# Last terms along w made inside the attention's first turns, position terms in row halves, q and k weights loaded two pairs ahead

## The chip, the cores and the metric

The kernel runs on one core of a Trainium2 chip. Its time is device microseconds of one execution. Its engines work beside each other: TensorE (PE in the profile; PEld is its weight load), VectorE (DVE), ScalarE (ACT), GpSimd (POOL), and SyncE (SP), whose queue issues nearly all DMAs, in order.

## The reference

Four layers follow each other on an input of 48 x 48 tokens with 768 channels, all in f32. Only the first, a transformer block, is touched; and of that, its attention:

```python
xn = layernorm(x, ln1_g, ln1_b)
qkv = xn.reshape(B, H * W, C) @ qkv_w + qkv_b              # 12 heads of 64
attn = jnp.einsum('bqc,bkc->bqk', q * scale, k)            # 2304 x 2304 for each head
rel_h = jnp.einsum('bhwc,hkc->bhwk', r_q, Rh)              # r_q is q as 48 x 48 rows; Rh, Rw are
rel_w = jnp.einsum('bhwc,wkc->bhwk', r_q, Rw)              # tables of relative positions
attn = attn + rel_h[:, :, :, :, None] + rel_w[:, :, :, None, :]
out = softmax(attn) @ v
```

Then come the projection, the residual, a second layernorm and the MLP. The other layers (two in the frequency domain, one of iterated convolutions) are as they were.

## The kernel before

**q, k and v.** `qkv_phase` goes through the tokens in three blocks of 768 (`sb`, three of `NSB`). Each product of 768 x 768 is made from seven half-size products instead of eight; their weights are prepared in the first block and kept in DRAM (`wqk_d`, `wv_d`). In a later block `v_rows` makes v first (L166), and `q_and_k` then makes q and k for six pairs of heads (`pr`, 128 channels each; L297). A pair's weights are one tile of 1344 KB, of which three are held. `v_weights` loads those of pairs 0 and 1; those of the others are loaded where the pair begins (L277). q, k and v go to DRAM (`q_d`, `k_d`, `v_d`). In the last block, after pair 1, `ahead(0)` loads the one-hot matrix and the first pair's keys and values for the attention (L331).

**Position terms.** For every query and head there are 48 terms along h and 48 along w. Each is f32, and is split by two ACT casts and two DVE subtractions into three bf16 parts whose sum it is (`split`, L369). One step of `rel_w` (four columns w, all pairs; L395) or `rel_h` (four rows h of one token half, two pairs; L409) is four f32 matmuls, eight passes on TensorE, followed by one split. A block has 12 steps of each kind. A step's table (192 KB, four held) is loaded by SP up to three steps ahead. `advance()` takes the next step: eight are taken between the passes of pairs 2 to 5, the rest in the next block's `v_rows`. In the last block the rest stands behind the last pair: the 4 last steps along h, then the 12 along w. The parts go to DRAM (`rh_d`, `rw_d`), from where the attention reads them.

**The bound.** Also behind the last pair, a small matmul (L477) yields a bound on the scores, from which `flag` follows. It chooses between `attention_bounded`, which runs here, and `attention_any`. What is inside the branch cannot mix with what is outside.

**The attention.** It works on a pair of heads at a time, one in partitions 0 to 63 and one in 64 to 127. The queries come in five chunks of 464 (the last has 448), the keys in 18 tiles of 128, three to a turn (`KB`). So there are 6 x 5 x 6 = 180 turns, numbered `i`. A turn is: three keys' products q.k (L576, f32, contraction over 64 rows, so that the two heads use the two row halves of the array), the terms for the same three (L585: a one-hot bf16 matrix of 120 rows times the bias tile of 120 rows, added in PSUM onto the product), exp on ACT (L587), row sums of the exps on DVE (L595), and the values of the turn before (L606, f32, 64 columns for each head). At a chunk's end the sums are added over partitions (L614), inverted (L616) and multiplied in (L622), into `oT`, the attention's output. [...]

`load_bias` lays out a chunk's bias tile: 120 rows are 48 for w (16 columns x 3 parts) and 72 for h (24 rows x 3 parts), for both heads, two halves of the key rows and three groups of columns. A chunk's loads are put into SP's queue when the chunk before begins; the next pair's keys and values at the pair's second chunk. Every sixth turn from the third on, a step of `weight_sums` is taken (`other`), which loads later weights, combines them on POOL and stores them; it uses slots of the exps' tile `p`, of which there are ten.

Of the kernel before, what the change touches and what calls it, by code (L numbers as in the profile page):

```python
# [20 lines left out]
P = 128  # L21
# [160 lines left out]

def qkv_phase(tc, ident, x, qkv_w, qkv_b, relT, rel_d, ln_g, ln_b, q_d, k_d, v_d, rw_d, rh_d, wqk_d, wv_d, flag, home, ahead):
# [18 lines left out]
    with (  # L202
# [67 lines left out]
        def q_and_k(sb, have_q, step):  # L270
# [4 lines left out]
            for pr in range(NC):  # L275
                if sb:
                    if (sb, pr) not in wqks:  # L277
                        load_qk(sb, pr)
                    w = wqks.pop((sb, pr))
                else:  # L280
                    w = w_tile(f"wqk_{sb}_{pr}").rearrange("p (n c f) -> p n c f", n=7, c=NC2)
                    wb = wp.tile([P, NC2, P], F32, tag="wb", name=f"wb_{pr}", bufs=2)
                    lo, hi = slice(pr * P, (pr + 1) * P), slice(C + pr * P, C + (pr + 1) * P)
                    nc.sync.dma_start(w[:, 0:2].rearrange("p a c f -> p (a c) f"), wv[:, :, lo])
                    nc.sync.dma_start(w[:, 6], wv[:, NC2:, hi])
                    nc.sync.dma_start(wb, wv[:, :NC2, hi])
                    combine(nc.gpsimd, (w[:, 0], w[:, 1], wb, w[:, 6]), w[:, 3], w[:, 2], w[:, 5], w[:, 4])
                    made.append(w)
                    if pr:
                        nc.sync.dma_start(wqk_d[pr - 1], made[pr - 1])  # L290
# [40 lines left out]
                if pr == 1 and sb + 1 == NSB:  # L331
                    ahead(0)
# [9 lines left out]
        with tc.tile_pool(name="qkv_v0", bufs=1, side="right") as vp:  # L342
            w = vp.tile([P, 7, NC2, TB], F32, tag="wv", name="wv")
            a21 = vp.tile([P, NC2, TB], F32, tag="a21", name="a21")
            load_x(0, 0)
            for k in range(2):
                nc.sync.dma_start(w[:, k], wv[:, k * NC2 : (k + 1) * NC2, 2 * C : 2 * C + TB])
            prepare(0, 0)
            load_x(0, 1)
            nc.sync.dma_start(w[:, 6], wv[:, NC2:, 2 * C + TB :])  # L350
            nc.sync.dma_start(a21, wv[:, :NC2, 2 * C + TB :])
            vb = load_bcast(nc, kp, qkv_b[2 * C : 3 * C], C, "vb")
            qkb = load_cols(nc, kp, qkv_b[0 : 2 * C], 2 * NC, "qkb")
            kb = kp.tile([P, NC], F32, tag="kb", name="kb")
            rel = qp.tile([P, 2, 2 * G - 1], F32, tag="rel", name="rel")
            for s in range(2):
                nc.sync.dma_start(rel[s * HD : (s + 1) * HD], relT)
            qms, kms = (qp.tile([P, NC, NSB], F32, tag=n, name=n) for n in ("qms", "kms"))
            prepare(0, 1)
            combine(nc.gpsimd, (w[:, 0], w[:, 1], a21, w[:, 6]), w[:, 3], w[:, 2], w[:, 5], w[:, 4])  # L360
            sums(0)
            V.tensor_scalar(kb, qkb[:, NC : 2 * NC], HD**-0.5, None, ALU.mult)
            v_rows(0, lambda n: w[:, n])
            nc.sync.dma_start(wv_d, w)

        with tc.tile_pool(name="qkv_o", bufs=1, side="right") as op:
            R = 2 * G

            def split(ps, parts, n):  # L369

                r = op.tile([P, TB], F32, tag="rest", name=f"rest_{n}", bufs=2)
                r = r[:R].rearrange("p (a b c) -> p a b c", a=ps.shape[1], b=ps.shape[2])
                nc.scalar.copy(parts[0], ps)
                V.tensor_tensor(r, ps, parts[0], ALU.subtract)
                nc.scalar.copy(parts[1], r)
                V.tensor_tensor(parts[2], r, parts[1], ALU.subtract)
# [7 lines left out]
            def position_terms(sb, q):  # L384


                q6 = q.rearrange("p c b (j w h) -> p c b j w h", j=KJ, w=KTW)
# [6 lines left out]
                def rel_w(g):  # L394

                    if g == 0:
                        tiles["rw"] = op.tile([P, 3, NC, 2, TB], BF16, tag="rw", name=f"rw_{sb}")
                    d, at = tiles.pop(("w", g)), tiles["rw"]
                    ps = pm.tile([P, 512], F32, tag="m", name=f"rw_{sb}_{g}")
                    pv = ps[:R, :TB].rearrange("p (c b w h) -> p c b w h", c=NC, b=2, w=4)  # L400
                    j, w0 = divmod(4 * g, KTW)
                    for i in range(4):
                        nc.tensor.matmul(pv[:, :, :, i, :], lhsT=d[:, i, :], rhs=q6[:, :, :, j, w0 + i, :], start=True, stop=True)
                    cols = slice(j * P + w0 * KTH, j * P + (w0 + 4) * KTH)
                    split(ps[:R, :TB].rearrange("p (c b t) -> p c b t", c=NC, b=2), [at[:R, n, :, :, cols] for n in range(3)], f"w{sb}_{g}")
                    if g == G // 4 - 1:
                        store(rw_d, at, slice(0, NC * TS))
# [23 lines left out]
                for g in range(G // 4):  # L431
                    steps.append((lambda g=g: load(("w", g), 1, g), lambda g=g: rel_w(g)))
# [33 lines left out]
            rm = qp.tile([P, 2], F32, tag="rm", name="rm")  # L466
            V.tensor_reduce(rm, rel, axis=AX.X, op=ALU.max, apply_absolute_value=True)
            V.tensor_scalar(km, km, rm[:, 0:1], rm[:, 1:2], ALU.add, ALU.add)
            pz = qp.tile([P, 2, NC], F32, tag="pz", name="pz")
            V.memset(pz, 0.0)  # L470
# [3 lines left out]
            onec = qp.tile([P, 1], F32, tag="onec", name="onec")  # L474
            V.memset(onec, 1.0)
# [5 lines left out]
            for _ in range(4):  # L481
                advance()
            inner.close()
            for _ in range(5):
                advance()
            ahead(1)
# [22 lines left out]

def queries(qc):  # L510

    return slice(qc * QB, min(T, (qc + 1) * QB))


def load_onehot(nc, pool, oneh_d, o):

    f = pool.tile([P, 3, P], F32, tag="onehf", name="onehf")
    nc.sync.dma_start(f[:NBR], oneh_d)
    nc.vector.tensor_copy(o[:NBR], f[:NBR])


def attention_loads(nc, q_d, k_d, v_d, rw_d, rh_d):
# [7 lines left out]
    def chunk(qb, c):  # L530
        pr, qc = c
        q = queries(qc)
        n = q.stop - q.start
        nc.sync.dma_start(qb[0][:, :n], q_d[pr * P : (pr + 1) * P, q])
        for s in range(2):
            load_bias(nc, qb[1][:, s, :, :, :n], rw_d, rh_d, 2 * pr + s, q.start, n)
# [4 lines left out]
def attention_bounded(tc, ahead, oT, beside, load_next):  # L541
# [14 lines left out]
    with (  # L556
# [22 lines left out]
        def scores(c, kt):  # L579
# [4 lines left out]
            for s in range(2):  # L584
                nc.tensor.matmul(ps[:, s, :n], lhsT=oneh[:NBR, b % 3, :], rhs=held(c)[1][:NBR, s, b // 3, j, :n], start=False, stop=True)  # L585
# [39 lines left out]
        other = beside(op, lambda name: pp.tile([P, 2, QB], F32, tag="p", name=name).rearrange("p a c -> p (a c)")[:, : 2 * TB].rearrange("p (a c) -> p a c", a=2))  # L625
        for i in range(len(work) + 1):
            if i % 6 == 3:
                next(other, None)
            if i == len(work) - 8:
                load_next()  # L630
            if i < len(work):
                c, k0 = work[i]
                pr, qc = c
                if k0 == 0:
                    nxt = (pr, qc + 1) if qc + 1 < NQB else (pr + 1, 0)
                    if nxt[0] < NC:
                        load_chunk(held(nxt), nxt)
                    if qc == 1 and pr + 1 < NC:
                        load_keys_values(kvs[(pr + 1) % 2], pr + 1)
                for kt in range(k0, k0 + KB):  # L640
                    products(c, kt)
                for kt in range(k0, k0 + KB):
                    scores(c, kt)
            if i:
# [3 lines left out]
                for kt in range(k0, k0 + KB):  # L648
                    values(c, kt)
                if k0 + KB == NT:  # L650
                    finish(c)
        for _ in other:
# [3 lines left out]
def attention_any(tc, ident, oneh, q_d, k_d, v_d, rw_d, rh_d, oT, beside, load_next):  # L656
# [4 lines left out]
    GQ = 2  # L661
    with tc.tile_pool(name="an_o", bufs=2) as op:
# [3 lines left out]
    with (  # L666
# [9 lines left out]
        nc.vector.memset(ones, 1.0)  # L676
        ka = cp.tile([HD, T], F32, tag="ka", name="an_ka")
# [633 lines left out]
def block_kernel(ctx: ExitStack, tc: tile.TileContext, a: dict):  # L1311
# [20 lines left out]
    oneh = atc.tile([P, 3, P], BF16, tag="oneh", name="oneh")  # L1332
# [4 lines left out]
    def load_ahead(stage):  # L1337
        if stage == 0:
            load_onehot(nc, atc, a["oneh"], oneh)
# [5 lines left out]
        qbs = [(pool.tile([P, QB], F32, tag=f"qt{i}", name=f"qt{i}"), pool.tile([P, 2, 2, KJ, QB], BF16, tag=f"bt{i}", name=f"bt{i}")) for i in range(2)]  # L1345
        loads[1](qbs[0], (0, 0))
        ones = pool.tile([P, HD], F32, tag="ones", name="ones")
        nc.vector.memset(ones, 1.0)
# [14 lines left out]
    pw, pw_close = opened("pw", [P, 2, NC2, TB], "right")  # L1363
    load_pw = lambda: nc.sync.dma_start(pw, ps_d[:, :2])
    bounded = nc.values_load(flag)
    with tc.If(bounded > 0) as which:
        attention_bounded(tc, ahead, oT, beside, load_pw)
    with which.Else():
        attention_any(tc, ident, oneh, q_d, k_d, v_d, rw_d, rh_d, oT, beside, load_pw)
# [487 lines left out]
```

## Time and profile before

| | us |
|---|---|
| median of 3 runs | 3815.2 (3811.54 to 3820.01) |
| profiled execution | 3815.61 |
| its span, first to last instruction | 3813.4 |
| mean granted TensorE clock | 0.987 of full |

The profile's page divides the span into 40 slices of 95.3 us. Each digit is the busy share of a slice in tenths:

```profile
PE   7999979999999999998999999999999998999998
DVE  6655455656566666565424433232325567995455
ACT  1323244444444444420310120011013356222342
DMA  7655563333332322124334534443454402112345
```

The attention is the stretch from the sixth slice to the eighteenth, in which ACT is at 4. Its matmuls and exps stand in the page's list of groups: line, engine, operation, output <- inputs, shape, count, then busy time and mean of one:

```profile
L576 PE MATMUL s<-qt,kv 64*128 64x464 f32 (+1 forms) x2160 | 467.8, 565 | 7.6 <-ACT p L587 5.4
L606 PE MATMUL av<-p,kv 128*64 128x464 f32 (+1 forms) x2160 | 456.3, 557 | 0.0
L585 PE MATMUL s<-bt,oneh 120*128 120x464 bf16 (+1 forms) x1080 | 241.3, 359 | 0.0
L587 ACT ACTIVATE p<-s 128x928 f32<-128x928 f32 (+1 forms) x540 | 467.9, 940 | 681.5 <-PE s L585 575.1
```

An f32 matmul is two passes, and each counts as one. A duration is that of one pass, from its start to its modelled end, and passes overlap; their pace is read from their starts.

### The profile page before, as it was taken

How to read it: one execution, taken by the hardware profiler on the slowest of the kernel's cores; microseconds unless marked ns; L12 is line 12 of the kernel's file. 1: busy time of each engine (PE TensorE's matmuls, PEld its weight loads, DVE VectorE, ACT ScalarE, POOL GpSimd, SP SyncE). 2: the span in 40 equal slices, each digit the busy share in tenths (PEclk: the TensorE clock that was granted, in tenths of full speed). 3: DMA queues.
4: the chain of work that ended last, by engine and by line, in shares of the span. 5: the costliest groups of instructions: out<-in, count | busy, mean ns of one | idle time of the engine just before them, and what ended most of it. 6: DMA issues, size and time to landing. Idle time of an engine off the chain costs nothing.

```text
span 3813.4 us, 51839 instructions
## 1 busy us (share of the span) xinstructions
PE 3707.4 (97%) x20914; PEld 2168.0 (57%) x20914; DVE 2032.0 (53%) x3070; ACT 1135.3 (30%) x1803; POOL 653.5 (17%) x498
## 2 busy tenths in 40 slices
PE   7999979999999999998999999999999998999998
PEld 4666543333333333345555555555568876996685
DVE  6655455656566666565424433232325567995455
ACT  1323244444444444420310120011013356222342
POOL 3101001111111111025000000000013301981131
PEclk9999989999999999999999999999999999999999
DMA  7655563333332322124334534443454402112345
GB/s 261 209 191 190 182 189 121 114 108 114 102 101 90 101 90 76 50 86 156 133 105 134 172 109 126 134 133 108 125 161 110 112 29 94 40 33 73 98 117 154
DMA packets 276271, 460.28 MB, mean 121 GB/s; under 512 B 50909, under 2 KB 228821, under 8 KB 269527
## 3 DMA queue, kind: packets, MB, share of 16 engines
q1 hardware_dynamic: 266215, 435.94, 37.5%
q10 hardware_dynamic: 9808, 20.94, 1.5%
q8 instruction: 167, 2.74, 0.3%
q14 instruction: 81, 0.66, 0.1%
HBM read 318.49 MB, written 138.31 MB: 120 GB/s over the span
## 4 chain that ended last, share of the span: by engine, by line
PE 87%; DVE 4%; POOL 3%; DMA 3%; ACT 1%; issue 1%; SPq 0%; ACTq 0%; POOLq 0%; DVEq 0%
PE p L886 13%; PE p L949 13%; PE s L576 12%; PE av L606 11%; PE qk L297 6%; PE s L585 6%; PE c L1113 4%; PE v L166 3%; POOL t L1214 2%; PE pj L166 2%; PE f_z L1516 2%; PE f_z L1517 2%; PE f_x L1481 2%; PE so L1291 2%; PE f_u L1531 2%; PE rh L417 1%
## 5 line engine op out<-in xcount | busy, mean ns | idle before, releaser
L595 DVE TENSOR_TENSOR acc<-acc,p 128x928 f32<-128x928 f32 (+1 forms) x480 | 561.6, 1170 | 359.4 <-ACT p L587 328.1
L587 ACT ACTIVATE p<-s 128x928 f32<-128x928 f32 (+1 forms) x540 | 467.9, 940 | 681.5 <-PE s L585 575.1
L949 PE MATMUL p<-w,h 128*128 128x384 f32 x1512 | 492.7, 486 | 0.0
L576 PE MATMUL s<-qt,kv 64*128 64x464 f32 (+1 forms) x2160 | 467.8, 565 | 7.6 <-ACT p L587 5.4
L606 PE MATMUL av<-p,kv 128*64 128x464 f32 (+1 forms) x2160 | 456.3, 557 | 0.0
L949 PEld LDWEIGHTS p<-w,h 128*128 128x128 f32 x1512 | 286.2, 190 | 196.9
L576 PEld LDWEIGHTS s<-qt,kv 64*128 64x128 f32 x2160 | 194.2, 187 | 277.5 <-issue 161.9
L886 PE MATMUL p<-x2nT,w 128*128 128x384 f32 x864 | 293.9, 490 | 3.3 <-issue 3.3
L606 PEld LDWEIGHTS av<-p,kv 128*64 128x64 f32 x2160 | 141.9, 136 | 247.1 <-issue 237.8
L297 PE MATMUL qk<-xnT,wqk 128*128 128x384 f32 x756 | 252.5, 491 | 5.0 <-DMA wqk<-wqk_d 5.0
L1206 PE MATMUL c<-H,bands 128*48 128x96 f32 x5632 | 243.8, 247 | 11.4 <-issue 10.9
L1206 PEld LDWEIGHTS c<-H,bands 128*48 128x48 f32 x5632 | 234.8, 123 | 20.6 <-issue 11.3
L585 PE MATMUL s<-bt,oneh 120*128 120x464 bf16 (+1 forms) x1080 | 241.3, 359 | 0.0
L886 PEld LDWEIGHTS p<-x2nT,w 128*128 128x128 f32 x864 | 165.4, 192 | 119.2 <-issue 6.1
L886 PE MATMUL p<-xT,w 128*128 128x384 f32 x648 | 220.8, 486 | 0.0
L297 PEld LDWEIGHTS qk<-xnT,wqk 128*128 128x128 f32 x756 | 144.6, 193 | 99.8 <-issue 8.3
L585 PEld LDWEIGHTS <-oneh 120*128 120x128 bf16 x1080 | 90.9, 98 | 190.8 <-issue 110.3
L925 POOL TENSOR_TENSOR rr<-rr,ml_b 128x1152 f32<-128x1152 f32 x12 | 31.5, 2622 | 955.6 <-DMA rr<-xr_d 863.6
L881 ACT ACTIVATE h<-h,ml_b 128x384 f32<-128x384 f32 x144 | 88.3, 614 | 346.6 <-DVE h L901 174.3
L1214 POOL TENSOR_TENSOR t<-s,c 128x768 f32<-128x768 f32 x80 | 144.5, 1832 | 179.5 <-DMA bands<-in_bands_dram 168.9
L886 PEld LDWEIGHTS p<-xT,w 128*128 128x128 f32 x648 | 123.1, 190 | 85.9
L616 DVE RECIPROCAL rec<-rs 128x464 f32<-128x464 f32 (+1 forms) x30 | 91.1, 3038 | 98.7 <-PE rs L614 98.7
(322 smaller groups left out, 4792.6 us busy)
## 6 DMA issues: line engine op xcount, KB each, us to landing
w<-w1s_d SPq DMA_DIRECT2D x36, 768.0 KB
w<-w2s_d SPq DMA_DIRECT2D x36, 768.0 KB
w<-w1s_d SPq DMA_DIRECT2D x36, 576.0 KB
w<-in_mlp_w_dram SPq DMA_DIRECT2D x27, 768.0 KB
wqk<-wqk_d SPq DMA_DIRECT2D x12, 1344.0 KB
yu<-f_ys SPq DMA_DIRECT2D x24, 672.0 KB
f_yt<-yu SPq DMA_DIRECT2D x20, 720.0 KB
yu<-f_us SPq DMA_DIRECT2D x18, 720.0 KB
```

The source lines that it names most:

```text
L166: nc.tensor.matmul(p[:, :TB], lhsT=rhs[n][:, c, t * P : (t + 1) * P], rhs=w[:, c, :], start=c == 0, stop=c == NC2 - 1)
L297: nc.tensor.matmul(p[:, :TB], lhsT=w[:, n, c, :], rhs=ops[sb][n][:, c, :], start=c == 0, stop=c == NC2 - 1)
L576: nc.tensor.matmul(ps[:, s, :n], lhsT=keys[pr % 2][rows, kt * P : (kt + 1) * P], rhs=held(c)[0][rows, :n], start=True, stop=False)
L585: nc.tensor.matmul(ps[:, s, :n], lhsT=oneh[:NBR, b % 3, :], rhs=held(c)[1][:NBR, s, b // 3, j, :n], start=False, stop=True)
L587: nc.scalar.activation(p, ps[:, :, :n], AF.Exp)
L595: nc.vector.tensor_tensor(probs[c], probs[c], p, ALU.add)
L606: nc.tensor.matmul(avs[c][rows, : size(c)], lhsT=vals[pr % 2][:, kt, rows], rhs=p[:, s, :], start=kt == 0, stop=kt == NT - 1)
L886: nc.tensor.matmul(p[:, :TB], lhsT=w[n][:, c, :], rhs=rhs[n][:, c, :], start=c == 0, stop=c == NC2 - 1)
L949: nc.tensor.matmul(ps[t][:, :TB], lhsT=hs[left, f][:, t * P : (t + 1) * P], rhs=wt[:, f % KW2, :], start=f == 0, stop=f == NF2 - 1)
L1113: nc.tensor.matmul(ps[:K, i, :n], lhsT=v[:, c, tok : tok + K], rhs=w[:, cc, c0 : c0 + n], start=cc == NC - 1, stop=cc == 0)
L1206: nc.tensor.matmul(ps[r0 : r0 + G, k // 4, cols], lhsT=bands[:, n - GC, i, :] if gr else bands0[:, n, i, :], rhs=H[:, n, :, d : d + NPR], ...
L1214: GP.tensor_tensor(t, sc[:, ch], c1[:, m0 : m0 + GC].unsqueeze(2).to_broadcast([P, GC, RR, NPR]), ALU.mult)
```

## The change

*Last terms along w.* In the last block `qkv_phase` makes no terms along w any more. A generator, `last_terms_w`, makes them inside the attention. It reads the last block's q again from `q_d`, into a part of `oT` that is written later, and keeps the parts in another part of it. Its first call loads q and three tables; each of the next twelve does one step. The calls come at turn 0 (loads), ahead of the values in turns 2 to 5, 7 to 11 and 13 (`mid`), and behind them in turns 8 and 10 (`end`). The sums' PSUM bank `rs` holds the products. The last step stores the parts to `rw_d`, those of pair 0 first. Chunk 3, the first one that reads them, is therefore loaded from turn 15 on instead of 12.

*Row halves.* The bias tile and the one-hot matrix are laid out anew: for each head, 64 of its 120 rows and then the other 56 stand in that head's row half. A key tile's terms are four matmuls, two of each half, and they follow the product of that key tile directly.

*Weights and other moves.* The weights of pair `pr + 2` are loaded at pair `pr`. `ahead(0)` moves from pair 1 to pair 4, `ahead(1)` and two of the steps along h move ahead of the bound's matmul, and the bound's constants to the first block. The first pair loads the next one's keys and values at its fourth chunk. The steps of `weight_sums` come at turns 15 + 28n/5.

```diff
+def last_terms_w(nc, oT, pool, psum, q_d, rel_d, rw_d):
+    sb = NTB // 2 - 1
+    ts = 2 * TB
+    q = oT[:, NC - 2 :].rearrange("p a t -> p (a t)").rearrange("p (c b t) -> p c b t", c=NC, b=2)
+    at = oT[:, 1 : NC - 2].bitcast(BF16).rearrange("p n (c b t) -> p n c b t", c=NC, b=2)
+    nc.sync.dma_start(q.rearrange("p c b t -> p c (b t)"), q_d.rearrange("(c p) t -> p c t", p=P)[:, :, sb * ts : (sb + 1) * ts])
...
+    for g in range(3):
+        load(g)
+    yield
+    for g in range(G // 4):
+        if g + 3 < G // 4:
+            load(g + 3)
+        r = pool.tile([P, TB], F32, tag="rest", name=f"restl_{g}", bufs=2)
+        terms_w(nc, tables.pop(0), q, at, g, psum(f"rwl_{g}"), r)
+        if g == G // 4 - 1:
+            for c0, c1 in ((0, 1), (1, NC)):
+                for s in range(2):
+                    nc.sync.dma_start(rw_d[s, :, :, sb, c0 * ts : c1 * ts], at[s * G : (s + 1) * G, :, c0:c1].rearrange("k n c b t -> k n (c b t)"))
+        yield
...
                 if sb:
-                    if (sb, pr) not in wqks:
-                        load_qk(sb, pr)
+                    if pr + 2 < NC:
+                        load_qk(sb, pr + 2)
...
-                if pr == 1 and sb + 1 == NSB:
+                if pr == 4 and sb + 1 == NSB:
                     ahead(0)
...
-                for g in range(G // 4):
+                for g in range(G // 4 if sb + 1 < NSB else 0):
...
+            advance()
+            advance()
+            inner.close()
+            ahead(1)
             ps = pm.tile([P, 512], F32, tag="m", name="bound")
...
-            for _ in range(4):
-                advance()
-            inner.close()
-            for _ in range(5):
-                advance()
-            ahead(1)
             while steps or ready:
                 advance()
...
+        for s in range(2):
...
+            p0 = s * HD
+            for a in range(2):
+                nc.sync.dma_start(dst[p0 : p0 + nw, a * KJ : (a + 1) * KJ], w)
+                nc.sync.dma_start(dst[p0 + nw : p0 + HD, a * KJ : (a + 1) * KJ], r[a, : HD - nw].unsqueeze(1).to_broadcast([HD - nw, KJ, m]))
+            nc.sync.dma_start(dst[p0 : p0 + NBR - HD, 2 * KJ :], r[:, HD - nw :].rearrange("a r t -> r a t"))
...
-            for s in range(2):
-                nc.tensor.matmul(ps[:, s, :n], lhsT=oneh[:NBR, b % 3, :], rhs=held(c)[1][:NBR, s, b // 3, j, :n], start=False, stop=True)
+            for k in range(2):
+                for s in range(2):
+                    rows = slice(s * HD, s * HD + (NBR - HD if k else HD))
+                    rhs = held(c)[1][rows, 2 * KJ + b // 3 if k else b // 3 * KJ + j, :n]
+                    nc.tensor.matmul(ps[:, s, :n], lhsT=oneh[rows, k, b % 3, :], rhs=rhs, start=False, stop=k == 1)
...
+        other_at = {15 + 28 * n // 5 for n in range(29)}
+        mid, end = {2, 3, 4, 5, 7, 8, 9, 10, 11, 13}, {8, 10}
         for i in range(len(work) + 1):
-            if i % 6 == 3:
+            if i in other_at:
                 next(other, None)
+            if i == 0:
+                next(terms)
...
-                if k0 == 0:
-                    nxt = (pr, qc + 1) if qc + 1 < NQB else (pr + 1, 0)
-                    if nxt[0] < NC:
-                        load_chunk(held(nxt), nxt)
-                    if qc == 1 and pr + 1 < NC:
-                        load_keys_values(kvs[(pr + 1) % 2], pr + 1)
+                nxt = (pr, qc + 1) if qc + 1 < NQB else (pr + 1, 0)
+                if k0 == (3 * KB if c == (0, 2) else 0) and nxt[0] < NC:
+                    load_chunk(held(nxt), nxt)
+                if k0 == 0 and qc == (1 if pr else 3) and pr + 1 < NC:
+                    load_keys_values(kvs[(pr + 1) % 2], pr + 1)
                 for kt in range(k0, k0 + KB):
                     products(c, kt)
-                for kt in range(k0, k0 + KB):
                     scores(c, kt)
+            if i in mid:
+                next(terms)
...
```

`terms_w` is the body of the old `rel_w`: four matmuls and the split, with its tiles given from outside. In `attention_any` the same generator runs through ahead of everything else.

## The prediction

> **What bounds the kernel now.** I read the page first: the busy table, then the chain that ended last.
>
> ```profile
> PE 3707.4 (97%) x20914; PEld 2168.0 (57%) x20914; DVE 2032.0 (53%) x3070; ACT 1135.3 (30%) x1803; POOL 653.5 (17%) x498
> PE 87%; DVE 4%; POOL 3%; DMA 3%; ACT 1%; issue 1%; SPq 0%; ACTq 0%; POOLq 0%; DVEq 0%
> ```
>
> TensorE is the bound, so a part of the change is worth what it takes from or adds to TensorE's own line, and the few idle gaps in it. The change touches the q/k stage (up to about 510 us) and the attention (512.66 to 1668.8 us). Everything behind stays.
>
> Next, one turn of the attention in the timeline of TensorE and its weight loads: start, duration, group (durations are modelled and overlap, so I subtract starts).
>
> ```profile
> 907.14 2.61 PE L576 MATMUL s<-qt,kv 64*128 64x464 f32 x12
> 909.68 1.35 PE L585 MATMUL s<-bt,oneh 120*128 120x464 bf16 x6
> 910.96 2.56 PE L606 MATMUL av<-p,kv 128*64 128x464 f32 x12
> 913.45 1.05 PE L576 MATMUL s<-qt,kv 64*128 64x464 f32 x4
> ...
> 900.66 0.19 PEld L576 LDWEIGHTS s<-qt,kv 64*128 64x128 f32 x2 [0.20 <-issue]
> 901.05 0.19 PEld L576 LDWEIGHTS s<-qt,kv 64*128 64x128 f32 x2 [0.20 <-issue]
> ...
> 909.89 0.10 PEld L585 LDWEIGHTS <-oneh 120*128 120x128 bf16 x1
> ...
> 910.09 0.10 PEld L585 LDWEIGHTS <-oneh 120*128 120x128 bf16 x1
> ```
>
> The products take 2.54 us, the terms 1.28, the values 2.49: 6.31 a turn, with no wait. The loads give the pace: a pair of f32 passes every 0.39 us (two row halves together), a bf16 terms pass every 0.195. Products and values are 6 pairs each, 2.34; terms are 6 passes, 1.17. So the change of kind costs 0.20 before products, 0.11 before terms, 0.15 before values. There are 180 turns (L585 x1080, six in each). In all, the attention has little else:
>
> ```profile
> 512.66:1668.80 1156.14, 1150.75 (x5512) 432.38 (x5514) 693.11 (x570) 469.50 (x542) 139.18 (x108) 1.00 0.33 98
> ```
>
> Columns from the window on: length, then busy time of PE, PEld, DVE, ACT, POOL. DVE works 60% of the stage, ACT 41%.
>
> Last, the three places where TensorE waits:
>
> ```profile
> 397.26 7.01 PE L297 MATMUL qk<-xnT,wqk 128*128 128x384 f32 x12 [5.04 <-DMA wqk<-wqk_d]
> ...
> 496.63 2.54 PE L403 MATMUL rw<-q,relD_w 128*96 128x96 f32 x16 [0.27 <-DMA relD_w<-in_relD_dram]
> 504.94 5.48 PE L403 MATMUL rw<-q,relD_w 128*96 128x96 f32 x40 [5.78 <-DMA relD_w<-in_relD_dram]
> 512.66 2.61 PE L576 MATMUL s<-qt,kv 64*128 64x464 f32 x12 [2.24 <-DVE rest_w L374]
> ...
> 553.64 3.73 PE L576 MATMUL s<-qt,kv 64*128 64x464 f32 x10 [3.65 <-ACT p L587]
> ```
>
> Brackets hold the idle time and what ended it. Each gap also costs clock: the granted clock was 0.50 from 396.3 to 403.1 and 0.54 from 553.6 to 557.0.
>
> **The change, part by part.**
>
> *Terms in row halves, product and terms alternating.* Per key tile two full-height bf16 passes become four half-height ones, two of each half. If the halves run together, this is again two passes of time. The f32 products show that they do: a 384-column full-height pass takes 0.323 (18 in the chain's 5.81), so 464 columns take 0.390, and a pair of halves takes 0.39. Twelve weight loads instead of six, 0.10 each, lie beside the passes; the next product's load (0.19) fits just into the last 0.195 pass. What goes is the step from half-height to full height before the terms, 0.11; the 0.20 and the 0.15 stay. 180 x 0.11 = **-19.8 us**. No row shows bf16 and f32 alternating within one geometry. Ends: all of the 0.11 gone, or a change of type costs as much as the present changes (second rival). The nearest row without a geometry change is free: at full height, 128 output rows after 96 start 0.68 us after eight 85-ns passes (341.71 to 342.39), so I take the full gain.
>
> Two rules of the Trainium skill bear on this. "TensorEngine Tiling (Array Packing)", Key Properties, says that a change of tiling mode drains the array, and nothing of types: by it, too, 19.8. "TensorE: Matmul & The Clock Gate", The mechanism, says that a weight load overlaps a running matmul only when its row group is another one. That speaks against the change: the six extra loads reuse a busy row group, and in three pairs they would add 3 x 0.10 a turn, +54 us, making this part +34. The rows above contradict it: loads of the same two halves follow each other every 0.39, exactly the matmuls' pace, so they lie hidden. I take the rows.
>
> *Last terms along w into the attention.* Between the last q/k pass (about 479.2) and the first terms of the attention (515.20) lie the bound's wait of 3.44, four steps along h, twelve along w with their table waits, and the split that frees PSUM. Afterwards only the four steps along h remain, two of them ahead of the bound. TensorE is through near 486 (four steps of 1.37, as from 332.13 to 333.50, somewhat more at half clock). What is late next is the first chunk's bias. Its tiles take memory that the last k store must leave; the trace has the memset of the ones, under the same wait, at 487.6. Then SP issues q and ten bias loads at 0.42 each (the rows of L505 and L506), to 492; loads issued there landed after 3 to 5 us, so terms can start at 496. Turn 1 would start 0.39 + 2 x (0.78 + 0.39) = 2.73 later, plus about 2.2 for the half clock after the idle stretch: 501, against 518.29 now (where exp's table load also held TensorE 1.7; with the first terms ahead of the second product that is hidden). **-17.3 us**; between -12 (loads as slow as the 512 to 530 stretch) and -21 (full clock).
>
> *What this adds.* Twelve steps run in turns 2 to 13: 0.68 of passes each (row above) and one more change of geometry, half height to full height and on, like the dearest one seen, 0.20: 12 x 0.88 = **+10.6 us**. Their two ACT casts (0.47, 0.51) and two DVE subtractions (0.55 each) fit the slack: a turn has 2.8 us of exp on ACT and 3.6 of sums on DVE in 6.3. q is read again, 2304 KB; at the 272 GB/s of 490 to 500 us that is 8.7 us from about 495.5, when SP has its branch behind it, and the first step asks for it near 511. Cover: two turns; without it TensorE waits, 1 to 5 us. Behind it on SP stand three tables and chunk 1's bias, due near 539, so they are hidden. The terms' store (2592 KB) leaves near 598, chunk 3's loads follow it on SP, due at turn 18 near 621; the store needs 10 us, the loads 5: hidden by some 8 us.
>
> *The q and k weights.* Pair 1's weights in the last q/k block came 5.04 late. SP's queue shows why:
>
> ```profile
> 372.50 0.59 SPq L528 DMA_DIRECT2D kv<-v_d  x1
> 373.18 3.04 SPq L392 DMA_DIRECT2D rw_d<-rw  x2
> 376.61 3.71 SPq L236 DMA_DIRECT2D v_d<-v_o  x1
> 380.37 3.73 SPq L247 DMA_DIRECT2D wqk<-wqk_d  x1
> ```
>
> The attention's values (1152 KB in 512-byte pieces) stand ahead of the weights. Loading two pairs ahead starts with pair 2, so it does not touch this load; the move of the attention's loads from pair 1 to pair 4 does, and takes about 1180 KB / 265 GB/s = 4.5 us or more out of the queue ahead. With the half clock (twelve passes in 7.01 where 12 x 0.323 and a tail make 4.1: 2.9) the gap costs 7.9. I take **-7.5**; ends 0 and -8. The moved loads, one-hot pieces and two weight loads pass SP's stores and tables of pairs 1 to 4; there the DMA share is 0.24 to 0.36, which hides them. Were it gone, a rh step waits for its table, up to 5.
>
> *The gap at 553.64.* An exp waited 9.57 for POOL, whose inputs lay behind the terms' store, bias and keys. The first weight sums move from turn 3 to 15, but store, chunk 3 and the next keys move there too. The gap costs 3.65 and about 1.5 of clock; I take half, **-2.5**, ends -5 and +4. DVE's moved constants and the smaller bias (1305 to 899 KB a chunk, ten issues instead of eight) are free: neither queue is late.
>
> Sum: -19.8 - 17.3 + 10.6 - 7.5 - 2.5 = **-36.5 us** on the profiled execution's 3815.6 (span 3813.4 and 2.2 around it): 3779.1. The median is 0.4 lower: **3779 us**.
>
> **Rivals.**
>
> 1. *The hand-over is not so smooth* (chance 0.18): the q reload, the bias or chunk 3 arrive late, or the exp's wait for POOL comes back whole. For it: the stretch from 512 to 560 was DMA-busy at 0.7 to 1.0, and 7 MB have to pass in turns 13 to 21. Against: 6 to 8 us of cover. Price 15: 3794.
> 2. *Types drain as geometries do* (0.09): with f32 and bf16 alternating, a turn pays 0.11 three times, 0.20 three times and 0.15, 1.08 instead of the 0.35 forecast: 180 x 0.73 = +131, so 3910, slower. It outweighs the rest from 36.5 / 180 = 0.20 a turn, that is 0.04 for each of the five added changes. For it: today's change into the terms is one of both type and geometry, so its 0.11 cannot be split. Against: the one change that is of geometry alone, values to products, is the dearest (0.20), so type adds nothing there that can be seen.
> 3. *The halves do not run together in bf16* (0.03): terms take 2.34 a turn instead of 1.17, +211: 3990. Against: f32 halves do.
>
> The forecast has 0.70. This measurement can tell a change from none at about 0.2%, 8 us. Faster by more: 0.70 and most of the 0.18, 0.85; within: 0.03; slower: 0.12. The range takes in the forecast's ends (-12 instead of -17.3, 0 instead of -7.5, +4 instead of -2.5 give 3798; the good ends 3772, and some for cheaper steps) and the first rival: 3763 to 3803.
>
> **What would show it.** A turn of 6.20 at full clock with product and terms groups 0.78 and 0.39 apart; turn 1 starting near 501 in the old count (near 493 with the weights' gap gone); twelve L403-like groups of 0.68 in turns 2 to 13; no gap at pair 1's weights. A turn above 6.31 proves the type rival; S groups of 0.78 the third; gaps in turns 2 to 20 the first.

## The result and the profile after

The changed kernel takes 3783.62 us (median of 4 runs, 3781.12 to 3785.74), where the kernel before, in 4 runs beside them, takes 3816.15. The ratio is 0.9914, with a 95% interval from 0.9899 to 0.9929: faster by 33 us. The profiled execution's span went from 3813.4 to 3779.3 us, at the same mean clock of 0.987; it is the fastest of the four. Busy time and the chain that ended last, from the page of the changed kernel:

```profile
PE 3691.0 (98%) x21994; PEld 2186.2 (58%) x21994; DVE 2039.8 (54%) x3073; ACT 1173.7 (31%) x1803; POOL 665.3 (18%) x498
PE 87%; DVE 4%; DMA 3%; POOL 2%; ACT 2%; issue 1%; SPq 0%; ACTq 0%; POOLq 0%; DVEq 0%
```

TensorE is still the bound. It has 1080 more instructions, the terms' second halves, and its busy time is 16 us less. A turn of the attention in TensorE's timeline (start, duration, group):

```profile
904.91 1.05 PE L650 MATMUL s<-qt,kv 64*128 64x464 f32 x4
905.79 0.56 PE L662 MATMUL s<-bt,oneh 64*128 64x464 bf16 x4
906.18 0.94 PE L650 MATMUL s<-qt,kv 64*128 64x464 f32 x4
906.97 0.56 PE L662 MATMUL s<-bt,oneh 64*128 64x464 bf16 x4
907.36 0.94 PE L650 MATMUL s<-qt,kv 64*128 64x464 f32 x4
908.14 0.56 PE L662 MATMUL s<-bt,oneh 64*128 64x464 bf16 x4
908.63 2.56 PE L683 MATMUL av<-p,kv 128*64 128x464 f32 x12
911.11 1.05 PE L650 MATMUL s<-qt,kv 64*128 64x464 f32 x4
```

The turn is 911.11 - 904.91 = 6.20 us. From terms to the next product it is 0.39 each time, two pairs of half-height passes; from a later product to its terms 0.79 or 0.78, two pairs of f32 passes. Nothing is lost where f32 and bf16 follow each other. The first product takes 0.88, with 0.10 of the change from the values in it.

The hand-over, from the last terms along h to the first step along w inside the attention, is in the same timeline:

```profile
482.71 2.63 PE L466 MATMUL rh<-q,relD_h 128*96 128x96 f32 x14
490.99 1.92 PE L650 MATMUL s<-qt,kv 64*128 64x464 f32 x4 [5.65 <-ACT rh L187]
492.67 1.19 PE L662 MATMUL s<-bt,oneh 64*128 64x464 bf16 x3
494.35 0.54 PE L662 MATMUL s<-bt,oneh 56*128 56x464 bf16 x1 [0.49 <-DMA bt<-rh_d]
...
498.37 1.03 PE L650 MATMUL s<-qt,kv 64*128 64x464 f32 x4
...
507.79 0.56 PE L662 MATMUL s<-bt,oneh 64*128 64x464 bf16 x4
508.28 0.92 PE L200 MATMUL rwl<-oT,relDl 128*96 128x96 f32 x8
509.13 2.56 PE L683 MATMUL av<-p,kv 128*64 128x464 f32 x12
```

Turn 1 starts at 498.37, where it started at 518.29. In two more profiles, of the changed kernel again and of its run with the loops exchanged (both below), it starts at 500.43 and 500.36. A step along w adds 509.13 - 508.28 = 0.85 us. The gap ahead of pair 1's weights, however, is still there, and so is what stands on SP's queue ahead of them:

```profile
373.01 0.59 SPq L601 DMA_DIRECT2D kv<-v_d  x1
373.69 2.84 SPq L447 DMA_DIRECT2D rw_d<-rw  x2
376.75 3.84 SPq L288 DMA_DIRECT2D v_d<-v_o  x1
380.65 3.77 SPq L299 DMA_DIRECT2D wqk<-wqk_d  x1
```

```profile
397.43 7.01 PE L349 MATMUL qk<-xnT,wqk 128*128 128x384 f32 x14 [4.72 <-DMA wqk<-wqk_d]
```

The terms of the prediction's sum, each read from starts in the two traces:

| | predicted | measured | from |
|---|---|---|---|
| type and geometry change, turns | -19.8 | -17.2 | 179 x (6.207 - 6.303) |
| hand-over, turn 1's start | -17.3 | -19.4 | 518.29 to 498.37, less 0.5 that came from earlier |
| twelve steps in the attention | +10.6 | +10.2 | 12 x 0.85 |
| q and k weights | -7.5 | -0.5 | last q/k pass 478.83 to 478.36 |
| gap at 553 | -2.5 | -5.2 | 3.65 idle and 1.5 of clock, all gone |
| what lies behind the last turn, rest | 0 | -2.0 | span less the rows above |
| sum | -36.5 | -34.1 | |

The table rests on one execution of each kernel. In the two more profiles the last q/k pass starts at 479.98 and 480.22, later than before the change, so the -0.5 of the q and k weights is no gain that can be relied on. Counted from that pass, the hand-over is worth 19.0 and 19.3 there, close to the 19.4 here. The stretch from the last turn's start to the end of the span is 1.9 shorter than before here, 2.6 shorter and 0.3 longer there, so the last row may be chance too.

### The profile page after: what moved, and what is told of

The parts are those of the page before. It is cut to its first block, busy times and chain, and to the rows that moved or that the text cites. A ratio compares the mean times of both kernels' runs of the same rounds, so it can differ in the third digit from the quotient of the medians.

```text
span 3779.3 us, 54106 instructions
## 1 busy us (share of the span) xinstructions
PE 3691.0 (98%) x21994; PEld 2186.2 (58%) x21994; DVE 2039.8 (54%) x3073; ACT 1173.7 (31%) x1803; POOL 665.3 (18%) x498
## 4 chain that ended last, share of the span: by engine, by line
PE 87%; DVE 4%; DMA 3%; POOL 2%; ACT 2%; issue 1%; SPq 0%; ACTq 0%; POOLq 0%; DVEq 0%
PE p L977 13%; PE p L1040 13%; PE s L650 12%; PE av L683 12%; PE qk L349 6%; PE s L662 6%; PE c L1204 4%; PE v L166 3%; PE pj L166 2%; PE f_z L1608 2%; PE f_z L1609 2%; PE f_x L1573 2%; PE so L1382 2%; PE f_u L1623 2%; POOL t L1305 1%; PE rh L466 1%
## 5 line engine op out<-in xcount | busy, mean ns | idle before, releaser
L664 ACT ACTIVATE p<-s 128x928 f32<-128x928 f32 (+1 forms) x540 | 506.5, 938 | 602.9 <-PE s L662 597.5
L650 PE MATMUL s<-qt,kv 64*128 64x464 f32 (+1 forms) x2160 | 528.9, 565 | 5.7 <-ACT rh L187 5.7
L662 PE MATMUL s<-bt,oneh 64*128 64x464 bf16 (+3 forms) x2160 | 302.6, 356 | 0.5 <-DMA bt<-rh_d 0.5
L662 PEld LDWEIGHTS <-oneh 64*128 64x128 bf16 (+1 forms) x2160 | 109.0, 93 | 260.5 <-issue 256.8
L1608 PE MATMUL f_z<-f_w,f_o 97*96 97x96 f32 x800 | 134.9, 250 | 0.0
```

The source lines that it names most:

```text
L650: nc.tensor.matmul(ps[:, s, :n], lhsT=keys[pr % 2][rows, kt * P : (kt + 1) * P], rhs=held(c)[0][rows, :n], start=True, stop=False)
L662: nc.tensor.matmul(ps[:, s, :n], lhsT=oneh[rows, k, b % 3, :], rhs=rhs, start=False, stop=k == 1)
L664: nc.scalar.activation(p, ps[:, :, :n], AF.Exp)
L1608: nc.tensor.matmul(out, lhsT=o1[:, j, 1:3, :].rearrange("c r h -> c (r h)"), rhs=w2t[:, b, 0, :], start=True, stop=False)
```

## The experiments

All times are medians, and ratios are to the kernel before in the same session. It took 3817.56 beside row halves alone, the rest alone, grouped and the exchanged loops; 3817.35 beside grouped with the steps later, both kernels with the terms along w first and the changed kernel again; and 3820.28 beside the other four.

**Row halves alone.** The kernel before, with the new bias tile, the terms in four half-height matmuls, and product and terms alternating. All else as before.

```diff
-            for s in range(2):
-                nc.tensor.matmul(... lhsT=oneh[:NBR, b % 3, :], rhs=held(c)[1][:NBR, s, b // 3, j, :n] ...)
+            for k in range(2):
+                for s in range(2):
+                    nc.tensor.matmul(... lhsT=oneh[rows, k, b % 3, :], rhs=rhs ...)
```

> The kernel before with the row halves alone: new layout of bias and one-hot, four half-height matmuls for a key tile, each directly behind its product. Last terms, weights and schedules stay as before. Theory (the change of geometry ahead of the terms goes, nothing else in the turn): a turn of 6.20 to 6.21 us instead of 6.31, 17 to 19 us less, 3797 to 3799. Rival (the turn is shorter only together with the new schedules, or half of its gain comes from elsewhere): no turn below 6.25, 3806 or more.

3801.14 us, 0.9956 [0.9942, 0.9969]. The usual turn is 6.207, so the halves bring the 0.096 a turn by themselves. In this kernel the exp's wait for POOL stayed, and grew (before: 3.65):

```profile
554.83 1.92 PE L609 MATMUL s<-qt,kv 64*128 64x464 f32 x4 [8.09 <-ACT p L623]
```

**The rest alone.** The changed kernel with the terms at full height, and with a turn's three products ahead of its three terms, as before.

> The changed kernel with the terms at full height again, three products and then three terms as before; the last terms along w, the weights and the schedules as changed. Theory (the parts add up): turns of 6.31 again, hand-over and terms as in the changed kernel, 15 to 18 us less than before, 3797 to 3801. Rival (the last terms need the shorter turn or the smaller bias tile to stay hidden): gaps in turns 0 to 18, less than 10 us gained, 3805 or more.

3812.89 us, 0.9988 [0.9979, 0.9996], from 13 runs between 3810.66 and 3818.92. The turn is 6.303, as before the change. But the gain is 5 us and not 15 to 18, and the two parts add up to 21, some 13 short of the changed kernel's 34 in that session. The timeline, of the slowest of these runs, has most of them in one place:

```profile
498.16 1.35 PE L660 MATMUL s<-bt,oneh 120*128 120x464 bf16 x6
511.66 0.93 PE L200 MATMUL rwl<-oT,relDl 128*96 128x96 f32 x4 [12.15 <-DMA relDl<-in_relD_dram]
512.52 2.69 PE L651 MATMUL s<-qt,kv 64*128 64x464 f32 x6
```

The first step along w stands right behind turn 0 here, not in turn 2 where the source puts it, and waits for its table, which follows the reload of q on SP. The instructions are put in order ahead of the run; with products and terms grouped, this step was placed ahead of turn 1. So the rival's number came, but neither the turn's length nor the size of the bias tile is the reason.

**Grouped.** The changed kernel, halves kept, with a turn's three products first and then the three terms.

```diff
                 for kt in range(k0, k0 + KB):
                     products(c, kt)
+                for kt in range(k0, k0 + KB):
                     scores(c, kt)
```

> The changed kernel with three products first and then the three key tiles' terms, still in row halves: two changes between f32 and bf16 a turn less on the way in and two less on the way back. Theory (a change of type costs nothing inside one geometry): turn of 6.20, time within 3 us of the changed kernel's 3783.6. Rival (each change of type costs a little, under what the timeline shows): faster by up to 180 x 4 x 0.01 = 7 us. Second rival (the early exp matters): TensorE waits for exp at turn starts, slower by over 5 us.

3799.32 us, 0.995 [0.9936, 0.9964]: 16 us are lost. Yet the usual turn is 6.209 with two changes of type in it instead of six. The loss is the same wait, and not one for an exp, as the second rival has it:

```profile
496.74 1.37 PE L662 MATMUL s<-bt,oneh 64*128 64x464 bf16 x12
509.48 1.56 PE L200 MATMUL rwl<-oT,relDl 128*96 128x96 f32 x8 [11.37 <-DMA relDl<-in_relD_dram]
```

**Grouped, with the steps later.** The kernel above; the first table's load also waits for an exp of turn 1, so that no step can be placed ahead of turn 1.

```diff
-        mid, end = {2, 3, 4, 5, 7, 8, 9, 10, 11, 13}, {8, 10}
+        mid, end = {4, 5, 7, 8, 9, 10, 11, 13}, {7, 8, 9, 10}
...
-            if i == 0:
+            if i == 2:
                 next(terms)
...
+        if late and g == 0:
+            nc.vector.tensor_copy(d[:1, 0, :1], late())
         nc.sync.dma_start(d, rel_d[1, g])
```

> The changed kernel with each turn's three products first and its three pairs of terms after them, and with the last terms' twelve steps in turns 4 to 13 instead of 2 to 13; the first table's load is held until turn 1 has made a row of weights, so that no step can stand ahead of turn 1. Theory: the change of type costs the pipeline nothing, and the 16 us that the grouped kernel lost were the wait of its first step for the reload of q. Then turns last 6.20 to 6.22 us, no wait for q appears, and the time is that of the changed kernel, 3780 to 3787 us. Rival: products and terms have to alternate, as the prediction took it, or grouping delays the exps; then about 3797 to 3800 us again.

3786.59 us, 0.9917 [0.99, 0.9933]; the changed kernel, run again beside it, took 3784.55. The wait is gone and 13 of the 16 us are back, so the wait was the loss and the changes of type cost nothing that shows. A little stays, which the alternating order does not have: TensorE waits 1.75 for an exp ahead of turn 1, and ten turns that follow a chunk's row sums last 0.1 to 0.7 longer (3.9 us in all from turn 15 on).

**The two halves of one head in succession.** The loops over halves and heads exchanged in the source.

> The changed kernel with another order in the four matmuls of a key tile's terms: both of the first head's half, then both of the second's, instead of taking turns. Theory (two halves run together only when neighbours in TensorE's queue are of different halves): the middle two overlap, the outer ones stand alone, 0.585 instead of 0.39 for a key tile, 180 x 3 x 0.195 = 105 us more, near 3889. Rival (each half works through its own queue, so order does not matter): 3784.

3783.34 us, 0.9908 [0.9893, 0.9923]. In the trace TensorE's passes stand in the new order in the first key tile alone, which waits for its bias; in the other 539 the two of 64 rows come first and the two of 56 after them, as in the changed kernel. So this says nothing of the order, which stays open; it is as good as a second run of the changed kernel.

**Weights as before.** Each pair's weights loaded where the pair begins, the attention's one-hot matrix, keys and values after pair 1.

```diff
-                    if pr + 2 < NC:
-                        load_qk(sb, pr + 2)
+                    if (sb, pr) not in wqks:
+                        load_qk(sb, pr)
...
-                if pr == 4 and sb + 1 == NSB:
+                if pr == 1 and sb + 1 == NSB:
                     ahead(0)
```

> The changed kernel with the q and k weights loaded where their pair begins and the attention's first loads placed at pair 1, both as before. Theory (these two moves change nothing that ends a wait: the values' load goes out when v is stored, wherever it is written): within 3 us of 3783.6. Rival (the earlier weights do save part of the gaps): 3 to 8 us slower than the changed kernel.

3782.66 us, 0.99 [0.9884, 0.9917], as the changed kernel. Both moves are worth nothing that shows. The trace says why of the second: the values' load leaves at 372.50 in the kernel before, at 373.01 in the changed one and at 373.64 in this one, each time as soon as v's first columns are stored. Only the keys' load moved, from 399.12 to 403.19.

**Values held.** A one-element copy from pair 4's q into the values' tile makes the load wait for that pair.

```diff
             kv_tile()
+            nc.vector.tensor_copy(kvs[0][:1, T : T + 1], after)
             loads[0](kvs[0], 0)
```

> The changed kernel, but the first pair's values are really loaded late: one element of their tile is written first from the q of pair 4, so the load cannot start before that. In the changed kernel's trace it still went out at 373.0, before pair 0. Theory (those 1152 KB stand in the DMA queue ahead of pair 1's weights): the gap of 4.7 at pair 1 shrinks under 1 and its half clock with it, 6 to 8 us less than the changed kernel, 3776 to 3778. Rival (the stores of v and of the terms ahead of the weights suffice for the delay): the gap stays over 3, time within 3 us of 3783.6.

3779.53 us, 0.9886 [0.987, 0.9903]. The load now leaves at 450.43, and still pair 1's weights are late:

```profile
396.88 1.61 PE L349 MATMUL qk<-xnT,wqk 128*128 128x384 f32 x2 [3.98 <-DMA wqk<-wqk_d]
```

In the other kernels that have the order of the changed one here, this idle time was 4.72 to 6.77, in one execution of each; in the two with the old order, before and row halves alone, it was 5.04 and 7.28. So the 1152 KB ahead of the weights cost TensorE some 0.7 to 2.8 us of the gap, not the whole. The gap is as the rival had it; the time, 4 us under the changed kernel's first median, lies between the two, and the intervals overlap.

**The terms along w first.** In each block the last four steps along h are put behind the twelve along w, so that the store of `rw_d` (2592 KB) leaves 17 us earlier; once with the values as they are, once with the values held.

```diff
+                h, wt = steps[n0 : n0 + 12], steps[n0 + 12 :]
+                steps[n0:] = h[:8] + wt + h[8:]
```

> The order of the terms alone, with the values' load as the changed kernel has it. Theory: the hole shrinks by some 1 to 3 us, since the store was ahead of the weights and the values' load still is: 3778 to 3783 us. Rival: the values' load alone keeps the hole at 4.5 us or more: 3783 to 3786 us.

> The changed kernel with the values' load held until pair 4 of the last block, and with a block's terms along w made ahead of its last four steps along h, so that their store (2 x 1296 KB) stands on SP's queue about 13 us earlier, where the DMA engines were 0.54 busy. Theory: the hole of 4 to 5 us ahead of the second pair's weights is the store's time on the DMA engines; without it and without the values' load the hole goes, and the half clock after it: 3771 to 3777 us. Rival: the values of the block (6 x 576 KB in rows of 1.5 KB) and the weights fill the DMA engines by themselves; the hole stays above 3 us and the time is that of the held values alone, 3778 to 3782 us.

3781.79 us (0.9907 [0.9891, 0.9924]) and 3781.25 us (0.9902 [0.9885, 0.9918]). The gap ahead of pair 1's weights is gone in both. The first time falls into its theory's range, but not for its reason; the second falls into its rival's range, though that gap did not stay. A larger gap appears earlier (7.37 and 7.25), shown for the kernel with the values held:

```profile
372.94 1.67 PE L466 MATMUL rh<-q,relD_h 128*96 128x96 f32 x8 [7.25 <-DMA relD_h<-in_relD_dram]
```

Now the tables of the steps along h come behind the store. The busy share of the DMA engines shows what both gaps have in common (length, busy PE, PEld, DVE, ACT, POOL, granted clock, DMA share, GB/s). A packet counts where it starts, so a share can pass 1. First the kernel with the values held alone:

```profile
360.00:370.00 10.00, 10.00 (x56) 6.98 (x55) 6.23 (x11) 3.78 (x8) 2.62 (x1) 1.00 0.54 202
370.00:380.00 10.00, 10.00 (x33) 5.89 (x32) 5.73 (x12) 0.68 (x2) 2.63 (x1) 1.00 0.86 206
380.00:385.00 5.00, 5.00 (x17) 2.88 (x16) 0.56 (x1) 1.09 (x2) 2.62 (x1) 1.00 0.97 263
385.00:390.00 5.00, 5.00 (x17) 3.01 (x16) 1.67 (x3) 0.34 (x1) 0.00 (x0) 1.00 0.98 292
...
395.00:400.00 5.00, 3.12 (x5) 1.82 (x6) 0.13 (x1) 0.00 (x0) 0.00 (x0) 0.69 1.00 410
```

The same view of the kernel with the terms along w first and the values held:

```profile
355.00:360.00 5.00, 5.00 (x24) 3.88 (x23) 2.60 (x5) 1.35 (x3) 0.00 (x0) 1.00 1.06 347
360.00:365.00 5.00, 5.00 (x22) 3.64 (x21) 2.13 (x4) 1.58 (x4) 1.75 (x1) 1.00 0.97 214
```

From the store on, the DMA engines are nearly full for 10 us and more, and what is due first behind it is late: the weights in one kernel, a table in the other. The stall was moved and not removed. Neither version is clearly faster than the changed kernel or than the held values alone: the intervals overlap.

**A tile of its own for the last terms along h.** Their parts get other memory, so that they need not wait for the store of the parts before.

```diff
-                        tiles["rh"] = op.tile([P, 3, 2, 2, TB], BF16, tag="rh", name=f"rh_{sb}_{cp}")
+                        if (sb, cp) == (NSB - 1, NC // 2 - 1):
+                            tiles["rh"] = op.tile([P, 3, NC, 2, TB], BF16, tag="rw", name=f"rh_{sb}_{cp}")[:, :, :2]
...
```

> The changed kernel with a tile of its own for the last four steps along h (that of the w terms, unused in the last block), so that their split need not wait until the tile before is stored. In the changed kernel ACT stood 6.3 us for that store and TensorE 5.65 us for ACT. Theory A (that store gates the hand-over): the split is done near 485, the first product moves to 487 to 488, the whole gains 3 to 5 us. Theory B (the first chunk's bias gates it: its last piece lands at 494.35 whatever the split does): first product earlier, terms not before 493.5, gain under 1.5 us.

3784.65 us, 0.9907 [0.989, 0.9923]: nothing, which of the two theories only B allows. The wait for ACT at the hand-over went, and the first chunk's loads took its place:

```profile
491.64 1.32 PE L653 MATMUL s<-qt,kv 64*128 64x464 f32 x4 [2.82 <-DMA qt<-q_d]
...
495.24 0.57 PE L665 MATMUL s<-bt,oneh 64*128 64x464 bf16 x2 [1.97 <-DMA bt<-rh_d]
```

**Weight sums as before.** A step of `weight_sums` at every sixth turn from the third.

```diff
-            if i in other_at:
+            if i % 6 == 3:
                 next(other, None)
```

> The changed kernel with the weight sums' steps at every sixth turn from the third on, as before. Theory (their late start keeps POOL's first sums off the crowded start; this removed the gap of 3.65 plus clock): an exp waits again for POOL near turns 6 to 8, 3 to 6 us slower. Rival (the gap went because the terms' store left the start): no gap, within 2 us of 3783.6.

3783.93 us, 0.9903 [0.9887, 0.992], and no gap near 553. With the sums where they were the gap is gone all the same; with the old place of the last terms and otherwise new halves (the first experiment) it is there. So the turn in which the sums begin is not its cause. What differs is SP's queue at the attention's start: the last input of POOL's first sum, `pw0b`, is issued at 545.52 in the first experiment's kernel and the sum starts at 551.86, where here they come at 521.73 and 527.16. Which of store, third chunk and keys stood ahead of it has not been tried.

**The changed kernel again**, beside the last three:

> The changed kernel unaltered, beside the three others on one chip. Both theories: 3781 to 3786 us, hole of 4.5 to 7 us ahead of the second pair's weights.

3784.55 us, 0.9913 [0.9896, 0.9929], with 5.38 idle ahead of pair 1's weights, where the first profile has 4.72. This gap differs from execution to execution by as much as the smaller effects looked for in it.

## Why the prediction held, and where it did not

The forecast was 3779; 3783.6 came, inside the range of 3763 to 3803, and on the side forecast. Of the 36.5 us, the three largest terms came nearly in size; the fourth was wrong. That the sum held so well is in part luck: the 7 us that did not come for the q and k weights were partly made up by 2.7 more from the gap at 553 and by 2 more from the hand-over.

**The turn: right, with luck in its size.** The turn became 0.096 shorter, where 0.11 was put: about what the step into the terms had cost. But the 0.11 was read from the wrong place. It is what the 1.28 from the terms' start to the values' start holds beyond its passes, and most of that is the step out of the terms, into the values. The step into the terms stands in the 2.54 ahead of it, as the kernel before shows in a narrow window:

```profile
909.19 0.56 PE L576 MATMUL s<-qt,kv 64*128 64x464 f32 x2
909.68 0.37 PE L585 MATMUL s<-bt,oneh 120*128 120x464 bf16 x1
```

The products' last pair takes 0.49 to the first terms pass, where the pace is 0.39, so the step into the terms cost about 0.10. The step out of them, from 910.67 to 910.96, takes 0.29 where a pass takes 0.196, and it is still there (908.34 to 908.63). The two happen to cost nearly the same, so the error did not show.

The second rival (types drain) falls: the grouped kernel has a third of the type changes and the same turn to within 0.002. (The added changes are four a turn, six against two, and not five, so its break-even would be 0.05 each.) The third falls as well: a pair of half-height bf16 passes takes 0.196. The rows of f32 weight loads were the right guide to the hidden loads, six more a turn, where the Trainium skill's rule on row groups ("TensorE: Matmul & The Clock Gate", The mechanism), taken by itself, would have made this part 34 us slower.

**The hand-over: right, but its cover was not.** Turn 1 came 2.6 earlier than the 501 of the sum, 0.5 of it from earlier stages; in the two more profiles it came 0.6 earlier. The last bias piece was there at 494.35, 2.6 after SP had issued it at 491.75; the sum took 3 to 5. The reload of q, however, was put 6.8 us clear of its use (from 495.5 for 8.7, asked for near 511). SP has the branch behind it at 494.98, about when the sum has it. But then the reload waits until the last terms along h are stored, a wait that the sum does not have (SP's waits from 494.95 to 498.1: in total, times, longest):

```profile
SPq L212 <- DMA rh_d<-rh: 2.9, 1, 2.9
```

It is issued at 498.05 and lands at 507.42; the first table behind it lands at 507.94; the step starts at 508.28. The cover was 0.34 us, and 1.63 and 0.63 in the two more profiles. The grouped kernel shows the price of a step placed before the landing, 11.4 us. So the first rival's mechanism was real, and the changed kernel missed it by little.

**The steps: right.** 0.85 each where 0.88 was put.

**The q and k weights: wrong.** The step that failed reads: "the move of the attention's loads from pair 1 to pair 4 does, and takes about 1180 KB / 265 GB/s = 4.5 us or more out of the queue ahead". It failed twice. First, the move in the program did not move the values' load: it left at 373.01 as soon as v's first columns were stored, and not where the source has it. The 372.50 in the prediction's own fence, ahead of pair 1's weights although the source has it after pair 1, showed this and was not read so. Second, even with that load taken away 3.98 of the gap stayed: the store of `rw_d` and those of v are then still ahead of the weights, with the DMA engines 0.86 to 0.98 busy from 370 to 390. The range's end at 0 for this term was the value that came.

**The gap at 553: right in direction, half in size.** Half was taken since the store, the third chunk and the keys move along, and all of it went. Not because they are out of POOL's way: in the changed kernel `pw0b` still stands right behind the terms' store (591.45 and 594.39) and POOL's first sum starts at 607.84, but no exp waits for it. Why none does has not been tried.

## What to carry over

A load is late or early by where it stands on its queue and by what its data wait for, so read the queue in the trace before a move in the source is given a price; to hold a load back, give it something to wait for. A stall behind a burst that fills the DMA engines can move to the next thing due when the burst is moved, as it did here. When work is brought into an early turn, ask what its inputs' load waits for, and compare their landing with the start of the use: here the cover was 0.3 to 1.6 us, and a step placed before the landing waited 11.4. And the time from a group's start to the next group's start holds the step out of the group, not the step into it.

## What the runs showed of the hardware

- Half-height bf16 matmuls of different row halves (64 rows, and also 56 rows) run beside each other: starts 7 ns apart, a pair every 0.196 us for 464 columns, as one full-height pass. Their weight loads, 0.09 each, go into a half that is at work and stay hidden.
- Going from f32 to bf16 and back within the halves costs nothing that starts show: 0.39 and 0.79 us from group to group, the passes alone.
- The granted clock was about half in the work that followed these idle stretches: 0.54 from 553.6 to 557.0 after 3.65 us (kernel before), 0.55 from 397.0 to 402.5 after 4.72 and 0.53 from 491 to 498 after 5.65 (changed kernel). After the gap of 4.72 the half clock lasted 4.6 us of work, so that gap cost about 7, an estimate (4.72 and half of 4.6).
- The DMA engines' busy share did not tell their rate. While the store of `rw_d`, in packets of 9216 bytes, was nearly all that moved, the engines were 0.97 busy at 214 GB/s (360 to 365 us, terms along w first and values held). When weights in packets of 10752 bytes were most of it, they moved 410 GB/s at a share of 1.00 (395 to 400 us, values held). The packets differ little in size, so that does not explain it; what does is open.
